# A third tile for layer 0's outputs, a store moved behind an activation, and four places in the order of layer 1's start changed

## The chip, the cores and the metric

The kernel runs on one NeuronCore of a Trainium2 chip. The metric is the device time of one execution in microseconds (us). The engines are named as the profile names them: PE (matrix multiply) with its weight loads PEld, DVE (vector), ACT (activation), POOL (GpSimd) and SP (which here only issues DMAs).

## The reference

The input x is fp32 of 4 images, 64 channels, 256 x 256. Two layers are computed, one after the other, each with a residual:

```python
    # --- layer 0 (conv_preact) ---
    x = x + _L0_conv_ref(_gn(x), ...)
    # --- layer 1 (conv_preact) ---
    x = x + _L1_conv_ref(_gn(x), ...)
```

`_gn` is a group norm over 32 groups of two channels: per image and group a mean and a variance over all pixels. Layer 0 is a 3x3 convolution with gelu, a 1x1 convolution to 128 channels that are split into xa and k, a 1x3 and a 3x1 depthwise convolution on xa with another gelu (the result is xs), a gate from the mean of xs over the image (softmax over three experts, the best two kept), three low-rank experts (ranks 2, 4 and 8) from k and xs, and a 1x1 projection:

```python
    h = _gelu(_conv2d(x, c1_w, ((1, 1), (1, 1))) + c1_b[None, :, None, None])
    h = _c1x1(h, c2_w, c2_b)
    xa, k = jnp.split(h, 2, axis=1)
    xs = _conv2d(xa, sh_w, ((0, 0), (1, 1)), groups=C) + sh_b[None, :, None, None]
    xs = _conv2d(xs, sv_w, ((1, 1), (0, 0)), groups=C) + sv_b[None, :, None, None]
    xs = _gelu(xs)
    ...
    return _c1x1(out, proj_w, proj_b)
```

Layer 1 is two 3x3 convolutions with quantized weights, each with a batch norm over all four images:

```python
    h = _conv3x3(x, _quantize_weight(w1), b1)
    h = jax.nn.relu(_batchnorm(h, gamma1, beta1))
    h = _conv3x3(h, _quantize_weight(w2), b2)
    h = _batchnorm(h, gamma2, beta2)
    return jax.nn.relu(h + identity)
```

## The kernel before

The work falls into stages. First the statistics of image 0 are read. Then the front runs: 64 units, 16 for each image, each of 16 rows of layer 0. A unit loads x (L548), takes differences of its rows on POOL and ACT, multiplies them on PE into `ps_c` (L532 through `front_conv`), combines the products on DVE (`butterfly_a` to `butterfly_d`, L650 to L669), applies gelu on ACT (L677) and runs the vertical taps on PE into `ps_a` in two halves (sub 0 and 1). For each half ACT writes t from ps_a (L718), DVE adds the horizontal taps in three steps (L725, L733, L736), ACT applies gelu to give xs (L749), and ACT issues the DMA that stores xs to DRAM (L754, `xs_store`). Every two units a product of h (`front_k`) and one of xs (`front_q`, L787) give the experts' low-rank values, which are stored too (L798).

The gate of an image is known only when all its xs are. So the outputs of image b are made 20 units later, inside the units of the next image (`plan_out`), 1 chunk of 16 rows (k from 0 to 15) per unit: SP loads xs (L865), the low ranks (L875) and x itself into a tile y (`out_load`, L855 and L856); PE projects into `ps_o` (`out_open`), in two halves n; DVE adds the projection to y (`out_add`, L901) and takes statistics of it (L906); SP stores y (`out_store`, L914). The y tiles have the tag "o" in the pool `work`, with two buffers, so the load of chunk k goes into the tile of chunk k - 2 and waits until that has been stored. While the front of image b runs, the statistics rows of image b + 1 are loaded as well (L429). The outputs of image 2 beyond the 22nd half and all of image 3 are made during layer 1 (`plan_out_late`).

The group norm of layer 1 is a chain of small steps with waits between the engines (`out_end`, through `group_norm`, `combine` and `root`): statistics are joined on DVE, PE sums them over partitions (`ps_m_y`, L283), DVE takes mean and differences (L285 to L290), PE sums again (`ps_v_y`, L293), DVE starts an inverse root (L296, L270, L271), POOL refines it in three steps (L275 to L277), and one operation makes the shift gn2[:, 2:3] (L924: on POOL for images 0 and 1, on DVE for 2 and 3). Each `next` of the chain has its own place in the order.

Layer 1's first convolution (`plan_conv1`) follows image by image, with 16 chunks and one last row each. For a chunk, SP loads the normalized-to-be rows yn (L933), POOL takes differences d (L362), ACT scales the odd rows in place and copies them (`conv1_upper_odd`, L951 and L378), ACT and DVE split the differences into two parts (L365, L372), DVE the odd rows (L381), PE multiplies them into `ps_hm` (odd) and `ps_h` (L315), ACT and DVE write the result h (L331, L337), ACT squares it for the batch norm (L401) and stores it. After the last chunk `conv1_end` (L1021) makes one more row, `ps_h_end`. Then comes the second convolution and a last pass over the output.

PSUM is cut into four banks of 4 KB per partition: two with the tag "c" (ps_c, ps_h), one "a" (ps_a, ps_hm) and one "p" (ps_o, ps_k, ps_q, ps_m_y, ps_v_y and others).

The order on every engine, and of the DMAs on SP and ACT, is written out by hand: `at(step, order, call)` enters a call under a step and an order within it, `at_slot(u, pos, call)` does it for a unit (two steps per unit), and all calls are run in sorted order with the scheduler told to keep that order on all five engines (L1320). `TAIL` gives the places of the units after the last one. The engines run in order: an instruction that waits holds all that stand behind it on its engine.

Of the kernel before, what the change touches and what calls it, by code (L numbers as in the profile page):

```python
# [9 lines left out]
F32 = mybir.dt.float32  # L10
# [4 lines left out]
ALU = mybir.AluOpType  # L15
# [5 lines left out]
P = 128  # L21
# [21 lines left out]
def conv_preact_kernel(ctx: ExitStack, tc: tile.TileContext, io, col128, colset, col64):  # L43
# [12 lines left out]
    def bank(tag, name):  # L56
        return psum.tile([P, 2, GP, W], F32, tag=tag, name=name, bufs=BANKS[tag])
# [53 lines left out]
    def chunk_out(name, tag, bufs):  # L111
        return work.tile([P, CPAIR, W], F32, tag=tag, name=name, bufs=bufs)
# [10 lines left out]

    eps = const.tile([P, 1], F32, name="eps")
    nc.vector.memset(eps, GN_EPS)
    eps_bn = const.tile([P, 1], F32, name="eps_bn")
    nc.vector.memset(eps_bn, BN_EPS)
    zeros = const.tile([P, PW], F32, name="zeros")
    nc.vector.memset(zeros, 0.0)
    m128 = const.tile([P, io["m128"].shape[1]], F32, name="m128")  # L130
# [1 line left out]
    def c128(name):  # L132
        return m128[:, col128[name][0] : col128[name][1]]
# [4 lines left out]
    av = lconst.tile([P, 3, C], F32, name="av")  # L138
    sv_sum, sh_sum, sh_bias, tap_bias = (column(n) for n in ("sv_sum", "sh_sum", "sh_bias", "tap_bias"))
    end, ends, edge_bias = column("end", 2), column("ends", 2), column("edge_bias", 2)  # L140
    outer = lconst.tile([P, 2, W], F32, name="outer")
    u_raw = lconst.tile([P, 6, 3, C], F32, name="u_raw")
    wk = lconst.tile([P, 2, 2, 32], F32, name="wk")
    both = lconst.tile([P, P], F32, name="both")
# [30 lines left out]
    def weights():  # L175

        m64_t = work.tile([P, 2, GF], F32, tag="xs", name="m64", bufs=4)
        m64 = flat(m64_t)[0:C, 0 : io["m64"].shape[1]]
        n = io["mc1"].shape[1]
        taps = flat(work.tile([P, 2 * GP, W], F32, tag="t", name="taps", bufs=1))[:, 0:n]  # L180
        nc.sync.dma_start(taps, io["mc1"])
        nc.sync.dma_start(m64, io["m64"])
        nc.sync.dma_start(m128, io["m128"])

        def c64(name):
            return m64[:, col64[name][0] : col64[name][1]]

        front_weights(taps)
        n = 9 * C
        nc.vector.tensor_tensor(flat(av), taps[:, n : n + 3 * C], taps[:, n + 3 * C : n + 6 * C], ALU.mult)  # L190

        nc.vector.tensor_reduce(sv_sum, c128("sv"), AX.X, ALU.add)
        nc.vector.tensor_reduce(sh_sum, sh, AX.X, ALU.add)
        nc.vector.tensor_scalar(sh_bias, sh_sum, c128("c2_ba"), c128("sh_b"), ALU.mult, ALU.add)
        nc.vector.tensor_scalar(tap_bias, sv_sum, sh_bias, c128("sv_b"), ALU.mult, ALU.add)
        for i in range(2):
            nc.vector.tensor_scalar(end[:, i : i + 1], sh[:, 2 * i : 2 * i + 1], c128("c2_ba"), None, ALU.mult)
        nc.vector.tensor_scalar(ends, end, sv_sum, None, ALU.mult)
        nc.vector.tensor_scalar(edge_bias, ends, -1.0, tap_bias, ALU.mult, ALU.add)
        for i in range(2):  # L200
            o = outer[:, i, :]
            nc.vector.tensor_scalar(o, zeros[:, 0:W], sh_bias, None, ALU.add)
            nc.vector.tensor_tensor(o[:, 0 : W : W - 1], o[:, 0 : W : W - 1], end, ALU.subtract)
            nc.vector.tensor_scalar(o, o, c128("sv")[:, 2 * i : 2 * i + 1], None, ALU.mult)

        nc.vector.memset(wk, 0.0)
        ps = small("ps_wk")
        nc.tensor.matmul(ps[:, 0:NLOW], c64("c2_k"), c64("w2_t")[:, 0:NLOW], start=True, stop=True)

        for s in range(2):  # L210
            half = slice(s * C, s * C + C)
            for i in range(2):
                o = 16 * i
                nc.vector.tensor_copy(wk[half, s, i, o : o + NLOW], ps[half, 0:NLOW])
        ps = small("ps_kb")
        nc.tensor.matmul(ps[:, 0:1], c64("w2_t"), c64("c2_bk"), start=True, stop=True)
        nc.vector.tensor_tensor(k_bias, ps[:, 0:1], c128("e_b2"), ALU.add)
        ps = small("ps_pw3")
        nc.tensor.matmul(ps[:, 0:C], c64("w3"), c64("proj_t")[:, 0:C], start=True, stop=True)
        nc.vector.tensor_copy(pw3, ps[:, 0:C])  # L220
        ps = small("ps_pb3")
        nc.tensor.matmul(ps[:, 0:3], c64("proj_t"), c64("b3"), start=True, stop=True)
        nc.vector.tensor_copy(pb3, ps[:, 0:3])
# [496 lines left out]
    def front_taps_h(u, sub):  # L720

        ps = open_a.pop((u, sub)).rearrange("p a b c -> p (a b) c")
        t = open_t[u, sub]
        edges = slice(0, W, W - 1)
        nc.vector.scalar_tensor_tensor(  # L725
            t[:, :, edges],
            ps[:, :, edges],
            sh[:, 1:2],
            edge_bias.unsqueeze(1).to_broadcast([P, 2 * GP, 2]),
            ALU.mult,  # L730
            ALU.add,
        )
        nc.vector.scalar_tensor_tensor(  # L733
            t[:, :, 1:W], ps[:, :, 0 : W - 1], sh[:, 0:1], t[:, :, 1:W], ALU.mult, ALU.add
        )
        nc.vector.scalar_tensor_tensor(  # L736
            t[:, :, 0 : W - 1], ps[:, :, 1:W], sh[:, 2:3], t[:, :, 0 : W - 1], ALU.mult, ALU.add
        )
        n = 2 * (u % NCH) + sub
        for at_n, i, row in ((0, 0, 0), (NOCT - 1, 1, 2 * GP - 1)):  # L740
            if n == at_n:
                rows = slice(i * C, i * C + C)
                nc.vector.tensor_tensor(t[rows, row, :], t[rows, row, :], outer[rows, i, :], ALU.subtract)

    def front_xs(u, sub):
        b, k = divmod(u, NCH)
# [105 lines left out]
        gate_engine.tensor_tensor(out_bias[b], row[:, 4:5], c128("proj_b"), ALU.add)  # L852

    def out_load(b, k):
        ys[b, k] = chunk_out(f"y_{b}_{k}", "o", 2)  # L855
        nc.sync.dma_start(flat(ys[b, k]), io["xp"][b, k])  # L856

    def xs_load(b, k, place):
# [161 lines left out]

    def conv1_end(b):  # L1021

        ps = bank("c", f"ps_h_{b}_end")
        convolve(ps[:, 0, 0, :], "w1", 0, diffs[(NCH - 1) % 2], CPAIR)
        h_out[b, NCH] = ps

# [51 lines left out]
    def at_each(places, chain):  # L1078
# [6 lines left out]
    SLOTS = UNITS + 3  # L1085

    TAIL = {
# [6 lines left out]
    }  # L1094
# [1 line left out]
    def at_slot(u, pos, call, *args):  # L1096

        step, order = (2 * u, pos) if pos < 6 else (2 * u + 1, pos - 6)
        if u >= UNITS:
            step, order = TAIL[u - UNITS, pos]  # L1100
            step += CONV1
        at(step, order, call, *args)

    def plan_front():
# [4 lines left out]
        for u in range(SLOTS):  # L1109
# [34 lines left out]
            if 0 <= u - 1 <= last:  # L1144
                at_slot(u, 7, front_taps_a, u - 1, 0)
                at_slot(u, 7.2, divide, u)
                at_slot(u, 9, front_taps_b, u - 1, 0)
                at_slot(u, 9.1, front_taps_i, u - 1, 0)
                at_slot(u + 1, 1.15, front_taps_h, u - 1, 0)
                at_slot(u + 1, 1.55, front_xs, u - 1, 0)  # L1150
                at_slot(u + 1, 1.6, xs_store, u - 1, 0)
            j = (u - 2) // 2
            alone = u < NCH + 4
            if u % 2 == 0 and 0 <= j < UNITS // 2:
# [104 lines left out]
    def plan_conv1(b):  # L1259
# [4 lines left out]
        for k in range(NCH):  # L1264
# [10 lines left out]

            at(load, 0, conv1_load, b, k)
            at(*late(diff, 13.08), conv1_differences, b, k)
            at(*late(odd, 13.36 if b == 0 and k == 3 else 13.1), conv1_upper_odd, b, k)
            behind = b == 0 and k == 1
            at(*late(up0, 13.36 if behind else 13.12), conv1_upper, b, k, 0)  # L1280
            at(*late(up1, 13.37 if behind else 13.14), conv1_upper, b, k, 1)
# [19 lines left out]
    for b in range(B):  # L1301
        if b < B - 1:
            plan_stats(b + 1)
            plan_out(b, NOCT if b < B - 2 else 22)
            if b == B - 2:
                plan_out_late(b, range(22, NOCT), [CONV1 + 16 + 4 * n for n in range(10)], 13.6, [(CONV1 + n, 12.6) for n in (56, 58, 58, 60, 60, 60, 61, 62)])
        else:
            t, e = CONV1 + 56, CONV1 + b * (NG + 1) - 10
            steps = [t + (e - 6 - t) * n // (NOCT - 1) for n in range(NOCT)]
            plan_out_late(b, range(NOCT), steps, 13.6, [(e - i, 15) for i in (5, 3, 3, 1, 1, 1, 0, -1)])  # L1310
        plan_conv1(b)

    kept_to = {
# [11 lines left out]
    def bn_affine(mv, gamma, beta, out, name):  # L1325

        ms = stat.tile([P, 2], F32, tag="ms", name=f"ms_{name}")
        for _ in combine(mv, B, c128("avg2"), eps_bn, ms, name):
            pass
        nc.vector.tensor_tensor(out[:, 0:1], ms[:, 1:2], c128(gamma), ALU.mult)  # L1330
        t = stat.tile([P, 1], F32, tag="s1", name=f"t_{name}")
        nc.vector.tensor_tensor(t, ms[:, 0:1], out[:, 0:1], ALU.mult)
        nc.vector.tensor_tensor(out[:, 1:2], c128(beta), t, ALU.subtract)
# [330 lines left out]
```

## Time and profile before

| what | us |
|---|---|
| median of 3 runs | 2936.22 |
| lowest and highest of them | 2935.35, 2952.88 |
| the profiled execution's own time | 2935.38 |
| its span | 2933.5 |
| PE busy | 2353.0 |
| DVE busy | 2435.1 |
| ACT busy | 1992.5 |
| POOL busy | 1693.0 |

The span is what the profile divides; 1.9 us of the execution's own time lie around it. The front's units run from about 62 to 1256 us, layer 1's first convolution from there to 1938, the second to 2497, the last pass to the end. Three kinds of views are used: windows (busy time of every engine in a stretch, with the granted clock, the share of time in which the 16 DMA engines were busy, and GB/s), the chain of waits (followed back from the last instruction of a window to what released it), and the timeline (instructions in order, with the idle time of the engine ahead of each in brackets and what ended it). Starts of the first butterfly operation on DVE (L650, once per unit) give the length of a unit.

### The profile page before, as it was taken

To read this page: it belongs to the slowest core of one execution; us is meant where nothing else is said; L and a number is where in the kernel's file an instruction comes from. 1 tells how busy PE (TensorE), PEld (TensorE's weight loads), DVE (VectorE), ACT (ScalarE), POOL (GpSimd) and SP (SyncE) were. 2 spreads that over 40 slices of the span, in tenths; PEclk is the share of its full clock that TensorE was granted. 3 is DMA by queue.
4 is the path that set the end of the run, shared out by engine and by line. 5 is a ranking of instruction groups with operands and counts; after the bars stand their busy time and mean duration, and the time that the engine had idled before them with its cause. 6 is when DMAs were issued, how large, how long until landed. Compare 5 with 4: busy or idle time off the path is not lost.

```text
span 2933.5 us, 52776 instructions
## 1 busy us (share of the span) xinstructions
PE 2353.0 (80%) x21576; PEld 1500.6 (51%) x21576; DVE 2435.1 (83%) x2818; ACT 1992.5 (68%) x2166; POOL 1693.0 (58%) x1315
## 2 busy tenths in 40 slices
PE   2999999999999999999899999989999999000000
PEld 1544445444445555456566667868888888000000
DVE  6788678888888988879998999879999898976664
ACT  4887887777775655576676677878888887432221
POOL 6999988787778888744454456735555564000000
PEclk9999999999999999999999999999999999555555
DMA  8665589999999999769999996657777764999999
GB/s 355 246 245 206 205 300 372 354 360 353 354 341 320 314 321 329 280 225 346 338 368 357 366 351 260 244 194 273 259 266 268 262 221 153 387 409 422 426 426 405
DMA packets 135715, 915.35 MB, mean 312 GB/s; under 512 B 14960, under 2 KB 15728, under 8 KB 40880
## 3 DMA queue, kind: packets, MB, share of 16 engines
q1 hardware_dynamic: 107824, 777.74, 71.3%
q10 hardware_dynamic: 27648, 134.23, 11.6%
q8 instruction: 170, 2.79, 0.4%
q14 instruction: 73, 0.60, 0.1%
HBM read 573.74 MB, written 338.17 MB: 311 GB/s over the span
## 4 chain that ended last, share of the span: by engine, by line
PE 48%; DMA 31%; DVE 11%; POOL 4%; ACT 3%; issue 2%; SPq 0%; ACTq 0%; DVEq 0%; POOLq 0%
PE ps_h L315 18%; PE ps_c L532 9%; DMA y<-in_xp 7%; DMA y_d<-y 6%; PE ps_h2m L315 6%; PE ps_a L532 6%; DMA y_end<-y_d 5%; DMA h<-h_d 4%; DMA out<-h 4%; PE ps_o L532 4%; PE ps_hm L315 3%; DMA yn<-y_d 3%; PE ps_q L787 1%; POOL x L580 1%; DVE y L901 1%
## 5 line engine op out<-in xcount | busy, mean ns | idle before, releaser
L315 PE MATMUL ps_h<-diff,w_q 128*128 128x512 f32 x3072 | 751.1, 399 | 7.6 <-DVE h L337 7.6
L315 PEld LDWEIGHTS ps_h<-diff,w_q 128*128 128x128 f32 x3072 | 574.3, 188 | 183.7 <-issue 24.5
L532 PE MATMUL ps_c<-v,us 64*64 64x256 f32 x9216 | 535.0, 380 | 13.8 <-DVE ps_c L663 11.3
L362 POOL TENSOR_TENSOR d<-yn 128x1024 f32<-128x1024 f32 x128 | 347.4, 2735 | 277.2 <-DMA yn<-y_d 181.1
L532 PEld LDWEIGHTS ps_c<-v,us 64*64 64x64 f32 x9216 | 358.7, 134 | 170.3 <-issue 15.8
L362 POOL TENSOR_TENSOR d<-h 128x1024 f32<-128x1024 f32 x126 | 307.7, 2464 | 206.5 <-DVE diff L370 136.9
L532 PE MATMUL ps_a<-h,av 64*64 64x512 f32 x4080 | 384.1, 490 | 35.4 <-DVE t L736 21.9
L337 DVE SCALAR_TENSOR_TENSOR h<-ps_h,scale_w,m 128x1024 f32<-128x1024 f32 x256 | 323.2, 1280 | 73.6 <-PE ps_h L315 59.3
L580 POOL TENSOR_TENSOR x<-x 128x512 f32<-128x512 f32 x256 | 328.9, 1285 | 12.8
L1526 ACT ACTIVATE h<-h,shift,gn 128x2048 f32<-128x2048 f32 (+1 forms) x65 | 134.3, 2067 | 274.5 <-DVE h L1525 269.9
L532 PEld LDWEIGHTS ps_a<-h,av 64*64 64x64 f32 x4080 | 152.9, 133 | 301.6 <-issue 194.6
L401 ACT ACTIVATE junk<-h,less_h 128x2048 bf16<-128x2048 f32 (+3 forms) x134 | 256.2, 1912 | 13.6 <-DVE h L337 13.5
L1525 DVE SCALAR_TENSOR_TENSOR h<-h,inverse,y_end 128x2048 f32<-128x2048 f32 (+1 forms) x65 | 150.5, 2317 | 120.5 <-DMA y_end<-y_d 120.5
L718 ACT ACTIVATE t<-ps_a,tap_bias,m 128x1016 f32<-128x1016 f32 x128 | 153.3, 1198 | 114.3 <-PE ps_a L532 85.2
L901 DVE SCALAR_TENSOR_TENSOR y<-ps_o,ob,y 128x1024 f32<-128x1024 f32 x128 | 163.9, 1280 | 50.7 <-PE ps_o L532 23.6
L749 ACT ACTIVATE xs<-t 128x1024 f32<-128x1024 f32 x128 | 134.8, 1053 | 104.0 <-DVE t L736 93.9
L315 PE MATMUL ps_h2m<-odd,w_q 128*128 128x512 f32 x768 | 193.2, 401 | 5.9 <-ACT odd L378 3.8
L315 PE MATMUL ps_hm<-odd,w_q 128*128 128x512 f32 x768 | 195.1, 404 | 2.8 <-DVE t L736 1.3
L372 DVE SCALAR_TENSOR_TENSOR diff<-d,gn,diff 128x1024 fp32r<-128x1024 f32 x128 | 192.7, 1536 | 0.0
L365 ACT ACTIVATE diff<-d 128x1024 fp32r<-128x1024 f32 x128 | 135.3, 1057 | 81.7 <-POOL d L362 80.1
L572 POOL TENSOR_TENSOR x<-x,x 128x512 f32<-128x512 f32 x128 | 160.8, 1278 | 21.3 <-ACT x L566 21.1
L315 PEld LDWEIGHTS ps_h2m<-odd,w_q 128*128 128x128 f32 x768 | 146.4, 191 | 42.6 <-ACT odd L378 3.9
(264 smaller groups left out, 4274.1 us busy)
## 6 DMA issues: line engine op xcount, KB each, us to landing
x<-in_xc SPq DMA_DIRECT2D x64, 1280.0 KB
h<-h_d SPq DMA_DIRECT2D x64, 1152.0 KB
yn<-y_d SPq DMA_DIRECT2D x60, 1152.0 KB
xs_in<-in_xp SPq DMA_DIRECT2D x64, 1024.0 KB
xs_d<-xs ACTq DMA_DIRECT2D x128, 512.0 KB
xs_in<-xs_d SPq DMA_DIRECT2D x64, 1024.0 KB
y<-in_xp SPq DMA_DIRECT2D x64, 1024.0 KB
y_d<-y SPq DMA_DIRECT2D x64, 1024.0 KB
```

Source lines behind the costliest of these rows:

```text
L315: nc.tensor.matmul(ps, wq[w][:, kind, kx, :], t[:, rows, kx : kx + W], start=(j == 0), stop=(j == len(terms) - 1))
L337: nc.vector.scalar_tensor_tensor(h.rearrange("p (e k) w -> p e (k w)", e=2), ps.rearrange("p e k w -> p e (k w)"), w_scale[w], m.unsqueeze ...
L362: engine.tensor_tensor(raw.rearrange("p (g r) w -> p g r w", g=2), *pair, ALU.subtract)
L365: nc.scalar.activation(inner(tiles[0], 4 * n, 4 * n + 4), raw, AF.Copy, scale=scale)
L372: nc.vector.scalar_tensor_tensor(lower, raw, scale, upper.bitcast(F32), ALU.mult, ALU.subtract)
L401: nc.scalar.activation(junk[rows, 0:n], flat(h), AF.Square, bias=less[name][rows], accum_out=total)
L532: last[:] = [nc.tensor.matmul(ps[o, at_out[0] : at_out[1], :], w[i], rhs[i], **flags)]
L572: nc.gpsimd.tensor_tensor(x4[:, j - 1], x_rows(u, j + 2), x4[:, j - 1], ALU.subtract)
L580: nc.gpsimd.tensor_tensor(x[:, r : r + 2], x[:, r + 2 : r + 4], x[:, r : r + 2], ALU.subtract)
L718: nc.scalar.activation(t[:, :, inside], ps[:, :, inside], AF.Identity, bias=tap_bias, scale=sh[:, 1:2])
L901: nc.vector.scalar_tensor_tensor(y, ps.rearrange("p x s w -> p x (s w)"), out_bias[b], y, ALU.add, ALU.add)
L1525: nc.vector.scalar_tensor_tensor(at_h, at_h, inverse[:, b : b + 1], y[:, a:e, :], ALU.mult, ALU.add)
```

## The change

Five edits and one tidying:

1. `out_load` takes every third chunk (k % 3 == 2) of images 0 and 1, and chunks 2, 5 and 8 of image 2, from a tile of its own with the tag "third" in the pool `front`, which has one buffer. The others stay on the two "o" tiles.
2. `xs_store` of the first half of a unit moves from place 1.6 of unit u + 1 to place 4.16, behind the second half's `front_taps_i` (4.15). `TAIL` is adapted.
3. `conv1_upper_odd` of image 0, chunk 0 moves from step t - 3 (unit 62's last places) to (t - 2, 4.2), inside unit 63, behind that unit's `front_taps_i`.
4. The chain of group norm 2 has its eight steps at 56, 60, 60, 64, 64, 66, 68 and 70 instead of 56, 58, 58, 60, 60, 60, 61 and 62; that of group norm 3 at e - 5, e - 2, e - 2, e + 1, e + 1, e + 1, e + 2 and e + 3 instead of e - 5, e - 3, e - 3, e - 1, e - 1, e - 1, e and e + 1.
5. `ps_h_end` goes to the bank "p" instead of "c".
6. `eps_bn` and `eps`, which are equal, become one tile; `outer` is kept as one row per partition, as only half of the partitions of each of its two rows was read.

Lines after L855 are three higher in the changed kernel (L924 becomes L927).

```diff
-    eps_bn = const.tile([P, 1], F32, name="eps_bn")
-    nc.vector.memset(eps_bn, BN_EPS)
...
-    outer = lconst.tile([P, 2, W], F32, name="outer")
+    outer = lconst.tile([P, W], F32, name="outer")
...
-                nc.vector.tensor_tensor(t[rows, row, :], t[rows, row, :], outer[rows, i, :], ALU.subtract)
+                nc.vector.tensor_tensor(t[rows, row, :], t[rows, row, :], outer[rows], ALU.subtract)
...
     def out_load(b, k):
-        ys[b, k] = chunk_out(f"y_{b}_{k}", "o", 2)
+        if k % 3 == 2 and (b < B - 2 or b == B - 2 and k < 11):
+            ys[b, k] = front_pool.tile([P, CPAIR, W], F32, tag="third", name=f"y_{b}_{k}")
+        else:
+            ys[b, k] = chunk_out(f"y_{b}_{k}", "o", 2)
         nc.sync.dma_start(flat(ys[b, k]), io["xp"][b, k])
...
     def conv1_end(b):
-        ps = bank("c", f"ps_h_{b}_end")
+        ps = bank("p", f"ps_h_{b}_end")
...
-        (0, 1.15): (0, 1.15), (0, 1.55): (0, 1.55), (0, 1.6): (0, 1.6), (0, 2): (0, 2), (0, 2.2): (0, 2.2),
+        (0, 1.15): (0, 1.15), (0, 1.55): (0, 1.55), (0, 4.16): (0, 1.6), (0, 2): (0, 2), (0, 2.2): (0, 2.2),
...
-        (1, 1.15): (3, 13.4), (1, 1.55): (3, 13.5), (1, 1.6): (4, 13.9), (1, 2): (5, 13.2), (1, 2.2): (5, 13.25),
+        (1, 1.15): (3, 13.4), (1, 1.55): (3, 13.5), (1, 4.16): (4, 13.9), (1, 2): (5, 13.2), (1, 2.2): (5, 13.25),
...
                 at_slot(u + 1, 1.55, front_xs, u - 1, 0)
-                at_slot(u + 1, 1.6, xs_store, u - 1, 0)
+                at_slot(u + 1, 4.16, xs_store, u - 1, 0)
...
-            at(*late(odd, 13.36 if b == 0 and k == 3 else 13.1), conv1_upper_odd, b, k)
+            at(*((t - 2, 4.2) if first else late(odd, 13.36 if b == 0 and k == 3 else 13.1)), conv1_upper_odd, b, k)
...
-                plan_out_late(b, range(22, NOCT), [CONV1 + 16 + 4 * n for n in range(10)], 13.6, [(CONV1 + n, 12.6) for n in (56, 58, 58, 60, 60, 60, 61, 62)])
+                plan_out_late(b, range(22, NOCT), [CONV1 + 16 + 4 * n for n in range(10)], 13.6, [(CONV1 + n, 12.6) for n in (56, 60, 60, 64, 64, 66, 68, 70)])
...
-            plan_out_late(b, range(NOCT), steps, 13.6, [(e - i, 15) for i in (5, 3, 3, 1, 1, 1, 0, -1)])
+            plan_out_late(b, range(NOCT), steps, 13.6, [(e - i, 15) for i in (5, 2, 2, -1, -1, -1, -2, -3)])
```

More of the change, by code (lines that the diff above doesn't have):

```diff
@@ L125, in conv_preact_kernel @@
     nc.vector.memset(eps, GN_EPS)
[L126 to L127 removed]
+    assert BN_EPS == GN_EPS
     zeros = const.tile([P, PW], F32, name="zeros")
@@ L200, in weights @@
         for i in range(2):
[L201 to L204, printed above, removed]
+            rows = slice(i * C, i * C + C)
+            o = outer[rows]
+            nc.vector.tensor_scalar(o, zeros[rows, 0:W], sh_bias[rows], None, ALU.add)
+            nc.vector.tensor_tensor(o[:, 0 : W : W - 1], o[:, 0 : W : W - 1], end[rows], ALU.subtract)
+            nc.vector.tensor_scalar(o, o, c128("sv")[rows, 2 * i : 2 * i + 1], None, ALU.mult)
         nc.vector.memset(wk, 0.0)
@@ L1327, in bn_affine @@
         ms = stat.tile([P, 2], F32, tag="ms", name=f"ms_{name}")
-        for _ in combine(mv, B, c128("avg2"), eps_bn, ms, name):
+        for _ in combine(mv, B, c128("avg2"), eps, ms, name):
             pass
```

## The prediction

> **What bounds the kernel now.** I read the page's busy shares and its slices first, since a share over the whole span mixes stages.
>
> ```profile
> PE 2353.0 (80%) x21576; PEld 1500.6 (51%) x21576; DVE 2435.1 (83%) x2818; ACT 1992.5 (68%) x2166; POOL 1693.0 (58%) x1315
> DMA  8665589999999999769999996657777764999999
> GB/s 355 246 245 206 205 300 372 354 360 353 354 341 320 314 321 329 280 225 346 338 368 357 366 351 260 244 194 273 259 266 268 262 221 153 387 409 422 426 426 405
> ```
>
> No engine is near 100%, but the DMA row has digits of 9 from the seventh slice on (a slice is 73 us), while the front still runs. The windows view of single stretches (PE, PEld, DVE, ACT, POOL busy, then clock, DMA share, GB/s) tells which stretch has which limit:
>
> ```profile
> 200.00:300.00 100.00, 96.19 (x1356) 50.54 (x1360) 80.43 (x122) 79.24 (x110) 90.16 (x78) 1.00 0.58 212
> 535.00:615.00 80.00, 75.43 (x1064) 39.71 (x1060) 66.54 (x91) 60.85 (x87) 62.74 (x68) 1.00 0.97 355
> 855.00:935.00 80.00, 79.73 (x1128) 40.85 (x1124) 70.55 (x94) 52.70 (x70) 66.40 (x72) 1.00 0.91 329
> 1300.00:1350.00 50.00, 49.80 (x242) 34.77 (x242) 44.66 (x63) 41.70 (x40) 25.15 (x11) 1.00 1.01 362
> 2500.00:2900.00 400.00, 0.00 (x0) 0.00 (x0) 281.97 (x134) 130.75 (x65) 0.00 (x0) 0.50 1.01 420
> ```
>
> From 855 on PE is full (79.73 of 80). At 535 to 615 PE is busy 75.43 of 80 and the DMA share is 0.97. Starts of one DVE operation per unit (L650) give the pace: from 426.8 to 863.4 us there are 22 units, 19.85 us each; just before and after, the chain has its PE pieces of ps_c 18.62 us apart (starts 404.08, 422.72, 441.33). So 22 x (19.85 - 18.62) = 27 us separate this stretch from PE's own pace, and no more can be won there. What ends last in it, the chain of waits says (start, length, what):
>
> ```profile
> 534.74 14.60 DMA y_d<-y
> 549.42 0.34 ACTq L754
> 549.81 1.21 ACT t L718
> ...
> 574.96 14.44 DMA y_d<-y
> 589.47 20.21 DMA y<-in_xp
> 609.76 1.28 DVE y L901
> ...
> 615.04 14.51 DMA y_d<-y
> ```
>
> Two things stand there. One is a loop over two `o` buffers: y store (14.4), y load into the same buffer (20.2), the add L901, and the store again, some 40 us for two units, which is what two units take. The other: at 549.42 ACT issues its xs store just as the y store of 534.74 lands. ACT sat behind a DMA completion, and t (L718) behind ACT.
>
> **The change part by part.** The sum goes against the profiled execution: span 2933.5, its own time 2935.4; the median of the runs shown is 2936.2, 0.8 above.
>
> *Third place for y, and xs store behind t (one gain, from units 21 to 43).* With three tiles in turn a y load no longer waits for the store two chunks before. SP waited 87.4 us for that in this stretch (L856 behind y_d, 21 times), but behind it SP waits for other things (L914 for the add L901, 84.3; L865, L429, L875 for other DMAs, 20 to 32 each), so only part moves forward. On DVE, L901 waited 14.7 us for y (9 times); on ACT, t waited 25.0 in 8 times under "PE ps_c" where the chain shows the DMA wait. These two are what can go: the store of the first half now stands behind the second half's t, where ACT's wait lies under DVE's three steps on t (0.23 + 1.28 + 1.28). All PE gaps of the stretch are 22.2 us, nearly all ps_a behind t. What is late next is the DMA itself: a unit moves 1280 + 4 x 1024 + 2 x 512 + 512 KB = 7.08 MB (page, part 6: x, stats rows, xs in, y, y_d, two xs halves, low ranks), which at PE's pace wants 380 GB/s. It has 355 at share 0.97, so some 366 at share 1, and 372 in the seventh slice: 19.0 to 19.3 us a unit. That is 0.5 to 0.85 us x 22 = 11 to 19 us if the queues never run dry. Ends: 0 (the pipe is the limit already) and -20 (372 GB/s kept). I take -10, below the middle, because the loads keep their order on SP behind the other waits. In units 43 to 62, PE is full and the same edit is worth 0. The xs store issues some 5 us later; its tile is reused two units (37 us) later, and the store lands 14 to 20 us after issue: hidden.
>
> The Trainium skill ("DMA: Bandwidth & Descriptors", section "Issuing engines are not separate DMA queues") says that transfers from SP and ACT share the same 16 engines, and that where they are issued only saves issue time. It speaks against this part: by it the stretch would keep its 355 GB/s and the sum would lose its -10. The share of 0.97 beside PE's 94% agrees with it halfway; the 0.03 left and the waits named above are what I count on.
>
> *Odd rows of layer 1 inside unit 63.* The timeline there:
>
> ```profile
> 1239.56 1.24 ACT L951 ACTIVATE yn<-yn,gn 128x1024 f32<-128x1024 f32 x1 [1.26 <-POOL d L362]
> 1242.40 0.70 DVE L650 TENSOR_TENSOR ps_c<-mc,ps_c 128x512 f32<-128x512 f32 x1 [2.22 <-ACT mc L645]
> 1246.66 4.22 PE L532 MATMUL ps_c<-v,us 64*64 64x256 f32 x48 [2.38 <-DVE ps_c L663]
> ```
>
> ACT waits 1.26 for POOL, does L951 and L378 (1.24 + 1.06), and only then mc, for which DVE and then PE wait; behind the 2.38 idle, 48 matmuls take 4.22 where they take 2.78 elsewhere (granted clock 0.69 in 1246 to 1251). The change puts L951 and L378 behind t. DVE then starts 2.2 earlier; PE's gap and slow restart are worth at most 2.38 + 1.44 = 3.8. Next late are the t steps and POOL's d, which PE waits for around 1268 (1.31) and 1291 (1.26), and the full pipe at 1300 to 1350 (share 1.01), so part is given back: -2.5 (0 to -3.8).
>
> *Chain of gn_2 spread (end of image 0 of layer 1).* Now PE waits at ps_m_y 1.86, ps_o 1.00, ps_v_y 2.82 (and 4.61 for 2.97 behind it), ps_h_end 1.26: 8.6 us. DVE sits 5.67 at L924. Afterwards L924 stands where POOL is long done (-5.67 on DVE), but ps_m_y and ps_v_y come right behind a ps_o, and ps_h_end too, all in the one `p` bank: each waits for the add L901. From DVE's rows (L901 1.28, behind L372 2.5 and L337 1.3) I get 3.7, 1.5 and 1.1, plus a slow restart of 1.5: 7.8. Between -1.5 and +2: 0.
>
> *Last row's bank, `c` to `p`.* At the end of image 1, ps_h_end waited 2.70 for DVE L337 and the next 12 matmuls took 4.14 instead of 2.97. In `p` it waits for L901 of the last output, done at 1627.26, so it starts 2.6 earlier; but the next ps_h waits for DVE's differences, which gain only the 0.27 wait and their order: -1.2 (-3.5 to 0). The skill ("Perfetto Trace Analysis", section "Optimizing Tensor Performance") wants independent matmul groups to rotate through banks, so that one is emptied while the next is filled. Going from two banks to a single one is against it, and by it this term would be 0 or a loss; here L901 ends before L337 does.
>
> *Chain of gn_3 later (start of image 3).* Now:
>
> ```profile
> 1783.85 10.89 POOL L362 TENSOR_TENSOR d<-yn 128x1024 f32<-128x1024 f32 x4
> 1784.32 0.20 DVE L924 TENSOR_SCALAR gn<-gn 128x1 f32<-128x1 f32 x1
> 1787.66 1.28 DVE L337 SCALAR_TENSOR_TENSOR h<-ps_h,scale_w,m 128x1024 f32<-128x1024 f32 x1
> 1790.04 1.24 ACT L951 ACTIVATE yn<-yn,gn 128x1024 f32<-128x1024 f32 x1 [3.73 <-POOL d L362]
> 1791.37 5.82 PE L315 MATMUL ps_h<-diff,w_q 128*128 128x512 f32 x24
> ```
>
> In the new order DVE's L271 comes behind d_15_0 (about 1785.0); POOL does two Newton steps (1.0 each), L939 (1 to 2.2), d_0_0 and d_0_1 (2.72 each), and only then the third step (0.9): 1794.4 to 1795.6. DVE's L924 waits for that, from about 1787 on, and behind it stand L337 of h_14 (1787.66 now, about 1795 then). PE's ps_h_15_0 waits for that bank: 1796.2 instead of 1791.4, and restarts slowly (+1.4). Given back: ps_h_end in `p` loses its 2.29 and the slow 4.50 behind it. From 1796.2: 4.4 + 2.9 for the two ps_h, 0.98, 2.97: ps_h_0_0 at 1807.3, now 1804.6: +2.7. A gap of 1.34 at ps_v_y (1776.9) goes, most of it under DVE. I take +2.5; ends -1 (DVE had slack) and +6 (nothing given back). PE is at 100% with the DMA at 0.72 behind this, so the loss stays.
>
> *Nothing:* one memset less, `outer` on halves (start, once), memory of the third tile (free before layer 1's pool opens), L951's new place at other images (none).
>
> Sum: -10 - 2.5 + 0 - 1.2 + 2.5 = -11.2: 2924.2 as profiled, 2925 as median.
>
> **Rivals.**
> *A: the pipe is the bound already.* For: 0.97 and 9s all along. Against: 1.01 at 1300. Then the front gives 0 to -3 and the rest -1.2: 2932 to 2935.
> *B: PE's full pace is reached.* For: both waits on the chain are taken away. Against: 380 GB/s were not seen in any front slice (372 at most). Then -27 - 1.2: 2908.
> *C: slower, by DVE's wait for POOL at 1787.* For: L924 is in order in front of h_14, POOL has 7.7 us of d_0 and L939 in front of its last step. Against: the two banks of `c` and ps_h_end in `p`. At its full price (+8, nothing given back) it decides when the front gives less than 6: with A, 2935.4 - 3.7 + 8 = 2940.
> *D: y is read from a tile whose place in SP's order is unchanged,* so it lands as late as before; only the xs store acts, half of the waits on the chain: -5 - 1.2: 2929.
>
> **How the numbers follow.** Forecast (front -6 to -16) 0.5: 2919 to 2929, 2925 as the likeliest. A 0.18, B 0.09, C 0.1, D 0.13. The range 2911 to 2938 leaves out B and the upper half of C, some 2 in 10 with what I have not thought of. The likeliest's own range is 2919 to 2929. About 1% (29 us) is what a measurement here tells from no change: faster by that needs more than B: 0.06; slower by that is out of reach of C: 0.03; within 1%: 0.91.
>
> **What would show it.** Pace of L650 between 427 and 863: 19.85 now, 19.4 by the forecast, 19.8 by A, 18.6 by B; GB/s there 364, 356, 380. SP's L856 no longer waiting for y_d. At unit 63 ps_c without a wait over 1 us, 48 matmuls in 2.8. DVE's L924 of gn_3 (L927 there) with an idle of 7 to 9 us behind POOL, and PE's ps_h idle 4 to 5 there. It is wrong if the pace stays and something else in SP's queue takes L856's place, or if the third image's start shows no idle of DVE.

## The result, and the profile after

| | before | changed kernel |
|---|---|---|
| median of 22 runs each, us | 2944.91 | 2943.93 |
| lowest and highest | 2935.35, 2952.98 | 2937.17, 2958.22 |
| ratio to before, 95% interval | | 1.0004 [0.9993, 1.0014] |
| profiled execution, own time and span | 2935.38, 2933.5 | 2941.94, 2939.8 |

No change in time can be told: the interval holds 1 (the quotient of the two medians is 0.9997). Of the three runs of before that the prediction had seen, two are the lowest of the 22, so their median, 2936.22, was low; the measured 2943.93 is above the forecast by 19 us, of which 8.7 are in the base and 10.2 in the change itself.

The two profiles, and all later ones, are compared by stretches. Each is the time between two starts on DVE: L650 of a unit (u), or L337 of the first convolution's n-th half chunk (h). "Before" is given for two profiles of it.

| stretch, us | before | changed | what lies there |
|---|---|---|---|
| u 0 to 18 | 310.7, 310.5 | 311.0 | front, PE bound |
| u 21 to 43 | 436.6, 436.8 | 441.7 | front with outputs and statistics loads |
| u 43 to 56 | 246.8, 246.8 | 247.5 | front, PE full |
| u 56 to h 0 | 160.2, 158.9 | 158.5 | unit 63's order |
| h 24 to 36 | 73.4, 72.9 | 72.3 | image 0's end, chain of gn_2 |
| h 56 to 72 | 88.5, 86.2 | 86.3 | image 1's end |
| h 88 to 96 | 39.9, 39.9 | 43.1 | image 3's start, chain of gn_3 |
| last h to the end | 439.3, 438.6 | 437.5 | second convolution's end, last pass |

The page of the changed kernel, in the lines that answer to those of before:

```profile
PE 2357.6 (80%) x21576; PEld 1498.7 (51%) x21576; DVE 2436.4 (83%) x2817; ACT 1991.8 (68%) x2166; POOL 1694.9 (58%) x1315
DMA  8665589999999999869999996647777764999999
GB/s 354 242 248 205 205 295 377 354 356 353 339 334 318 323 324 326 285 227 337 330 370 355 366 364 250 259 175 272 268 264 264 263 232 150 371 426 425 425 425 400
```

Hardly anything in it has moved. The windows view of a part of the stretch that was to gain (same columns as before):

```profile
535.00:615.00 80.00, 76.06 (x1068) 39.31 (x1064) 67.27 (x91) 60.73 (x87) 62.10 (x67) 1.00 0.96 352
```

352 GB/s where before had 355, and a share of 0.96 for 0.97. The y loads are free of the y stores. What SP waited for in units 21 to 43 (from 426 to 864 us; line, releaser, us in total, times, longest), first in the kernel before, then in the changed one, some rows of each:

```profile
SPq L856 <- DMA y_d<-y: 87.4, 21, 7.6
```

```profile
SPq L917 <- DVE y L904: 107.8, 22, 8.0
SPq L798 <- DMA ranks<-low_d: 32.2, 10, 4.8
...
SPq L859 <- DMA y<-in_xp: 23.8, 9, 3.1
...
SPq L548 <- DMA ranks<-low_d: 21.3, 9, 4.0
SPq L917 <- DMA y_d<-y: 21.0, 9, 2.8
...
SPq L859 <- DMA y_d<-y: 5.7, 1, 5.7
```

The wait of the y load for the y store is gone (87.4 us in 21 times before, one of 5.7 left). In its place stand waits of the y load, the low store, the x load and the y store for other DMAs that have not landed, and the y store waits longer for the add (107.8 us for 84.3). And DVE waits longer for y; the waits of the engines in the same window, before and changed:

```profile
ACT t L718 <- PE ps_a L532: 29.0, 28, 2.6
...
ACT t L718 <- PE ps_c L532: 25.0, 8, 3.4
...
DVE y L901 <- DMA y<-in_xp: 14.7, 9, 2.8
```

```profile
ACT t L718 <- PE ps_a L532: 43.9, 28, 3.3
DVE y L904 <- DMA y<-in_xp: 30.9, 10, 5.6
```

ACT's wait for a DMA ahead of t (25.0 us under "PE ps_c" before) has vanished as forecast, but t waits longer for ps_a (43.9 us for 29.0), and DVE waits 30.9 us for y, where it waited 14.7. The pace of units 21 to 43 is 441.7 / 22 = 20.08 us, not the 19.4 of the forecast: the pace did not fall and other DMAs took the place of L856's wait, which the prediction had named as the sign of its being wrong.

### The profile page after: what moved, and what is told of

The parts are those of the page before. It is cut to its first block, busy times and chain, and to the rows that moved or that the text cites. A ratio compares the mean times of both kernels' runs of the same rounds, so it can differ in the third digit from the quotient of the medians.

```text
span 2939.8 us, 52775 instructions
## 1 busy us (share of the span) xinstructions
PE 2357.6 (80%) x21576; PEld 1498.7 (51%) x21576; DVE 2436.4 (83%) x2817; ACT 1991.8 (68%) x2166; POOL 1694.9 (58%) x1315
## 3 DMA queue, kind: packets, MB, share of 16 engines
q8 instruction: 169, 2.77, 0.4%
## 4 chain that ended last, share of the span: by engine, by line
PE 47%; DMA 33%; DVE 10%; POOL 4%; ACT 3%; issue 2%; SPq 0%; ACTq 0%; DVEq 0%; POOLq 0%
PE ps_h L315 19%; DMA y<-in_xp 13%; PE ps_c L532 8%; PE ps_h2m L315 6%; PE ps_a L532 5%; DMA out<-h 4%; DMA y_end<-y_d 4%; PE ps_o L532 3%; DMA h<-h_d 3%; DMA yn<-y_d 3%; DMA y_d<-y 3%; PE ps_hm L315 3%; DMA xs_in<-in_xp 1%; POOL x L580 1%; DVE h L1536 1%
## 5 line engine op out<-in xcount | busy, mean ns | idle before, releaser
L315 PEld LDWEIGHTS ps_h<-diff,w_q 128*128 128x128 f32 x3072 | 577.2, 189 | 191.2 <-issue 19.7
L532 PE MATMUL ps_a<-h,av 64*64 64x512 f32 x4080 | 383.7, 489 | 27.2 <-DVE t L736 10.9
L337 DVE SCALAR_TENSOR_TENSOR h<-ps_h,scale_w,m 128x1024 f32<-128x1024 f32 x256 | 322.8, 1279 | 64.6 <-PE ps_h L315 51.5
L904 DVE SCALAR_TENSOR_TENSOR y<-ps_o,ob,y 128x1024 f32<-128x1024 f32 x128 | 164.0, 1281 | 76.2 <-DMA y<-in_xp 30.9
```

The source lines that it names most:

```text
L315: nc.tensor.matmul(ps, wq[w][:, kind, kx, :], t[:, rows, kx : kx + W], start=(j == 0), stop=(j == len(terms) - 1))
L337: nc.vector.scalar_tensor_tensor(h.rearrange("p (e k) w -> p e (k w)", e=2), ps.rearrange("p e k w -> p e (k w)"), w_scale[w], m.unsqueeze ...
L532: last[:] = [nc.tensor.matmul(ps[o, at_out[0] : at_out[1], :], w[i], rhs[i], **flags)]
L904: nc.vector.scalar_tensor_tensor(y, ps.rearrange("p x s w -> p x (s w)"), out_bias[b], y, ALU.add, ALU.add)
```

## The experiments

All times are ratios to runs of the kernel before on the same chip. "Stretch" is the time of units 21 to 43 in the one profile of each kernel, GB/s that of the window 430 to 840 us.

| kernel | ratio, 95% interval | stretch, us | GB/s |
|---|---|---|---|
| before, two profiles | | 436.6, 436.8 | 356, 357 |
| changed | 1.0004 [0.9993, 1.0014] | 441.7 | 352 |
| e1, statistics loads split | 1.0027 [1.0012, 1.0041] | 439.5 | 354 |
| e2, half statistics | 0.9946 [0.9926, 0.9966] | 418.9 | 345 |
| e3, chain of gn_3 as before | 0.9998 [0.9979, 1.0018] | 445.0 | 350 |
| e4, two y tiles | 1.0021 [1.0003, 1.0038] | 441.6 | 354 |
| e5, xs store as before | 0.9999 [0.9979, 1.0018] | 434.5 | 359 |
| e7, statistics earlier, gn_3 as before | 0.9985 [0.9971, 0.9999] | 427.1 | 352 |
| e8, three places as before | 1.0029 [1.0013, 1.0046] | 434.9 | 358 |
| e9, before with half statistics | 0.9939 [0.9920, 0.9958] | 420.8 | 344 |
| e10, y load first | 0.9990 [0.9976, 1.0004] | 433.7 | 359 |
| e11, e7 with xs store as before | 0.9963 [0.9945, 0.9981] | 424.9 | 355 |
| e12, gn_3 and xs store as before | 0.9996 [0.9979, 1.0013] | 435.9 | 358 |
| e13, before with statistics earlier | 0.9981 [0.9967, 0.9994] | 434.9 | 345 |
| e14, before with the later xs store | 1.0016 [1.0003, 1.0028] | 437.5 | 357 |
| e15, e13 with the third tile | 0.9970 [0.9958, 0.9983] | 424.8 | 355 |
| e16, e13 again | 0.9970 [0.9953, 0.9987] | 429.0 | 351 |

Three theories of the stretch were held against each other: *pipe* (the bytes that the DMA engines move are the bound), *in-flight* (the number of DMAs under way is the bound, since each waits for one issued eight before), and *loop* (the two y tiles are the bound, as the prediction had it). For *in-flight*: the DMAs carry eight semaphores in turn, and the waits of a DMA for another one that the trace of the changed kernel tells in this stretch (47 of them) are all for one issued seven to nine places before.

**Bytes or number of DMAs: e1 and e2.** e1 cuts the statistics loads of images 2 and 3 into two DMAs each, e2 leaves out the second of the two and takes the statistics of the first half twice, so that the engines do the same work.

```diff
+        n = CPAIR * W // 2 if b >= 2 else CPAIR * W
+        for a in range(0, CPAIR * W, n):
+            nc.sync.dma_start(flat(x_in[b, k])[:, a : a + n], io["xp"][b, k][:, a : a + n])
```

> The changed kernel, with every load of statistics rows of images 2 and 3 (units 12 to 43) cut into two DMAs of half a row each: one DMA more per unit (9.5 for 8.5), the same bytes. Theory pipe (units 21 to 43 are bound by the bytes that the 16 DMA engines move, some 355 GB/s): pace stays 20.0 to 20.2 us a unit, time within 5 us of the changed kernel. Theory in-flight (the trace shows that a DMA is issued only when the one issued eight before it has landed; that is what took the place of the y wait): eight in flight cover less, so 5 to 12% longer units: +20 to +50 us.

> The changed kernel, with only the first half of each load of statistics rows of images 2 and 3 (it leaves out half of these rows, the statistics are taken over the other half twice): 512 KB of 6912 KB less per unit in units 12 to 43, the same number of DMAs, waits and engine work. Theory pipe: 6.55 MB at 355 to 366 GB/s is 17.9 to 18.5 us, below PE's 18.62, so the stretch falls to PE's pace: -25 to -33 us, about 2912. Theory in-flight: one DMA of seventeen lands some 6 us earlier every second wait, the others as before: -3 to -10 us.

With one DMA more per unit the stretch took 439.5 us, not longer than the changed kernel's 441.7, where *in-flight* asked for 20 us more: it is out. (The whole of e1 is 0.0023 above the changed kernel; its profile has 1.6 us of that in units 0 to 18 and as much in 18 to 21, and 4.7 in the last pass, which e1 does not touch.) With 512 KB less per unit the stretch fell by 22.8 us. The windows view of e2 from 430 to 840 us, and of the changed kernel, the same:

```profile
430.00:840.00 410.00, 404.74 (x5672) 207.85 (x5664) 361.63 (x467) 330.88 (x467) 341.44 (x349) 1.00 0.96 345
```

```profile
430.00:840.00 410.00, 390.22 (x5415) 198.52 (x5404) 343.05 (x445) 316.15 (x446) 325.98 (x335) 0.99 0.97 352
```

PE is busy 404.74 of 410 in e2 and 390.22 in the changed kernel; the GB/s go down because PE now sets the pace. Note the share: 0.96 at 345 GB/s, 0.97 at 352. It does not tell which of the two kernels is bound by the pipe.

**Was the y loop ever a bound: e9 and e4.** e9 is the kernel before, with two y tiles, and e2's cut. e4 is the changed kernel without the third tile.

```diff
-        if k % 3 == 2 and (b < B - 2 or b == B - 2 and k < 11):
-            ys[b, k] = front_pool.tile([P, CPAIR, W], F32, tag="third", name=f"y_{b}_{k}")
-        else:
-            ys[b, k] = chunk_out(f"y_{b}_{k}", "o", 2)
+        ys[b, k] = chunk_out(f"y_{b}_{k}", "o", 2)
```

> The kernel before (two y tiles, early xs store), with only the first half of each load of statistics rows of images 2 and 3 (it leaves out half of these rows). Theory pipe: the loop of y store, y load and add was only the place where the full pipe showed; with 512 KB less per unit it shrinks by itself, and units 21 to 43 take 419 to 422 us as in the changed kernel with the same cut: -16 to -18 us. Theory loop (two tiles bind, whatever the bytes): the loop's 40 us for two units stays within 1 us, 430 us or more for the stretch, and the third tile is worth 10 us here: -5 us at most.

> The changed kernel, with all y tiles on the two old places. Theory pipe: the third place is worth nothing, time and pace of units 21 to 43 (20.0 to 20.2 us) stay, within 4 us. Rival (the third place helps and another edit of the front, the later xs store, costs as much): +5 to +10 us. Second rival (a third tile makes the queue deeper and so slower): -5 us, pace back to 19.85.

e4's stretch is the changed kernel's (441.6 and 441.7); the whole of e4 is 0.0017 above the changed kernel, with intervals that overlap, and this stretch does not show why. e9 falls to 420.8 us, and it still has the loop. The wait of its SP for y stores and the windows view, both from 430 to 840 us:

```profile
SPq L858 <- DMA y_d<-y: 86.0, 21, 7.0
```

```profile
430.00:840.00 410.00, 402.76 (x5664) 209.68 (x5660) 359.31 (x464) 329.61 (x466) 338.49 (x347) 1.00 0.95 344
```

SP waits 86.0 us for the y stores, no less than the kernel before does in this window (79.8 us in 20 times), with PE at 402.76 of 410, where before has this:

```profile
430.00:840.00 410.00, 388.84 (x5444) 199.20 (x5440) 344.45 (x448) 317.68 (x447) 328.45 (x338) 1.00 0.97 356
```

So this wait, read off the chain as the thing to remove, costs next to nothing. The transfers of the loop hardly became shorter in e9 (stores of 13.3 to 13.9 us and loads of 19.7 to 20.2 in its chain, 14.3 to 14.6 and 19.9 to 20.8 before), but the chain leaves it: y loads and y stores are 33.5% of the chain from 500 to 700 us in e9, and 87.0% of that from 480 to 640 in the kernel before.

**The y load's place in SP's order: e10.** `at_slot(u - 1, 2.0, out_load, b, k)` becomes `at_slot(u - 1, 0.1, ...)`.

> The changed kernel, with the y load first in SP's order of a unit, ahead of the loads of low ranks, xs and statistics rows instead of behind them (rival D of the prediction: y has lain at the same place of SP's order, so it landed as late as before). Theory pipe: y lands earlier, another load later, stretch of units 21 to 43 within 434 to 446 us, time within 4 us of the changed kernel. Rival D: DVE no longer waits for y (30.9 us there) and the stretch falls by 5 to 10 us.

DVE no longer waits for the y load, as rival D wanted, and the stretch is 433.7 us, 8.0 less than the changed kernel's, which is the size that rival D named. But other things come later in return: ACT's t waits 55.7 us for ps_a (426 to 864 us), and PE 10.9 us for xs rows (430 to 840 us). Nor do 8 us of one profile decide: e3 and e8, which run the changed kernel's program up to unit 62, took 445.0 and 434.9 us. The ratio's interval holds 1; a gain of more than 0.24% on the kernel before is excluded, a smaller one is not.

**The xs store: e5, e12 and e14.** e5 and e12 take the store back to place 1.6 (e12 the chain of gn_3 too), e14 makes that edit alone on the kernel before.

```diff
-                at_slot(u + 1, 4.16, xs_store, u - 1, 0)
+                at_slot(u + 1, 1.6, xs_store, u - 1, 0)
```

> The changed kernel, with the first half's xs store back ahead of the second half's t. Theory pipe (bytes bound units 21 to 43): the stretch from unit 21 to 43 stays at 437 to 445 us and the time within 4 us of the changed kernel, though ACT's wait for a DMA ahead of t comes back. Rival 1 (ACT's wait was a real cost): +5 to +8 us. Rival 2 (the later store has made the queue worse, as the stretch was 436.6 us before and 441.7 after): -5 us, 436 us for the stretch.

> The changed kernel with two edits undone, those that the runs speak against: group norm 3's chain at its old places and the xs store ahead of t. By the profiles: -3 for the chain, 0 to -7 for the store: 0.997 to 1.000 of the time before. Rival (the difference of 434.5 and 441.7 us was scatter and the chain's stall is given back later): 1.000.

> The kernel before with one edit only: the first half's xs store behind t. Theory pipe without a cost of the late store: 436 us for units 21 to 43 (436.6 and 436.8 in the two profiles of before), time within 2 us. Rival (the late store itself is what costs, as the profiles with it had 441.6 to 445.0 us and once 434.9): 440 us or more and 1.001 to 1.003.

By e14 alone the later store costs 0.16% (interval from 0.03 to 0.28), though its stretch, 437.5 us, is not the 440 that this theory named. By e12, which has the third tile and not the later store, there is no gain on before. The stretch without the later store scatters from 434.5 to 436.8 us (four profiles with all bytes in the order of before) and with it from 433.7 to 445.0. That the store costs some us there is likely; how many is not settled. What it does to the waits is plain. In e14, from 426 to 864 us:

```profile
ACT t L718 <- PE ps_a L532: 43.1, 31, 2.7
DVE y L901 <- DMA y<-in_xp: 26.8, 10, 4.1
```

So the longer waits of the changed kernel (43.9 and 30.9) come with this edit alone, with two y tiles; e5 and e12, with the third tile and without the edit, have 31.3 and 30.7 ahead of t and 15.5 and 14.9 ahead of the add, as before. Ahead of t this holds in all profiles with all bytes: 39.8 to 55.7 us with the later store, 29.0 to 31.3 without. The wait for y is less sure (with the edit, e8 has 19.5 and e1 14.8). The later store has taken away ACT's wait for a DMA and put other waits in its place. Behind this stretch its price is clear of scatter: units 43 to 56 take 247.5 to 247.8 us in the nine profiles with the later store and 246.8 or 246.9 in the nine without, and from unit 56 to 63 it is 0.5 us more.

**How far a profile scatters: e6.**

> The kernel before, unchanged, for a second profile: how far the stretch of units 21 to 43 scatters by itself. If 436.6 and 441.7 us differ only by scatter, this one may lie anywhere between 434 and 445 us; if the change made the stretch longer, it lies within 2 us of 436.6.

436.8 beside 436.6 us for the stretch. These two lie close, but one program differs by more elsewhere: 434.9 and 429.0 us in e13 and e16, one kernel on two chips, and 441.7, 445.0 and 434.9 in the changed kernel, e3 and e8, which are the same up to unit 62. So in units 21 to 43 a difference of less than 10 us between single profiles tells nothing. The last pass, the same in every kernel, took from 435.9 to 446.6 us over all profiles.

**The chain of gn_3: e3.** The places of before in the changed kernel:

```diff
-[(e - i, 15) for i in (5, 2, 2, -1, -1, -1, -2, -3)]
+[(e - i, 15) for i in (5, 3, 3, 1, 1, 1, 0, -1)]
```

> The changed kernel, with the chain of group norm 3 at its old places. My step (DVE's shift operation waits 8.4 us behind POOL's differences, PE 4.9 us and a slow restart): the stretch from h 88 of layer 1's first convolution to h 96 loses 3 us, total -3. Rival (the stall lies beside other waits): 0. DVE's idle ahead of the shift operation of gn_3 goes in both.

h 88 to 96 went back from 43.1 to 39.9 us, and is 39.9 to 40.1 in every kernel with the old places and 43.0 to 43.4 in every one with the new. In the changed kernel:

```profile
1798.83 0.21 DVE L927 TENSOR_SCALAR gn<-gn 128x1 f32<-128x1 f32 x1 [8.36 <-POOL gn L277]
1798.96 1.28 DVE L337 SCALAR_TENSOR_TENSOR h<-ps_h,scale_w,m 128x1024 f32<-128x1024 f32 x1
```

```profile
1793.22 4.69 POOL L362 TENSOR_TENSOR d<-yn 128x1024 f32<-128x1024 f32 x2
1797.90 0.34 POOL L275 TENSOR_SCALAR root_y<-var_y,gn 128x1 f32<-128x1 f32 x1
```

```profile
1800.30 8.01 PE L315 MATMUL ps_h<-diff,w_q 128*128 128x512 f32 x24 [4.86 <-DVE h L337]
```

Read from below: PE waits 4.86 us for DVE's h, DVE stands 8.36 us at a 0.21 us operation, because POOL does two differences of 2.35 us each ahead of the last step of the root. The whole-time ratio (0.9998 for 1.0004) has the right sign and cannot tell 3 us.

**The three other places: e8.** Unit 63's odd rows, the last row's bank and the chain of gn_2 as before, in the changed kernel.

```diff
-            at(*((t - 2, 4.2) if first else late(odd, ...)), conv1_upper_odd, b, k)
+            at(*late(odd, ...), conv1_upper_odd, b, k)
-    ps = bank("p", f"ps_h_{b}_end")
+    ps = bank("c", f"ps_h_{b}_end")
-    (56, 60, 60, 64, 64, 66, 68, 70)
+    (56, 58, 58, 60, 60, 60, 61, 62)
```

> The changed kernel with three edits undone: layer 1's first odd rows behind unit 62 again, the last row in bank c, group norm 2's chain at its old places. By my steps: unit 56 to unit 63 takes 132 us (130.3 in the changed kernel), image 1's end from h 56 to h 72 88.5 (86.3), image 0's end from h 24 to h 36 73.4 (72.2): in sum +4 to +5 us. Rival (what is won there is waited for later): each of the three shows locally, but the time stays within 2 us.

u 56 to h 0 took 159.4 us (158.5 in the changed kernel), h 24 to 36 74.1 (72.3), h 56 to 72 87.2 (86.3): +3.6 in the three. The time says +0.25% (1.0029 for 1.0004, intervals that just touch). All profiles together, eight with the old places and ten with the new, say it better: 158.9 to 160.6 us for u 56 to h 0 with the old and 157.9 to 158.5 with the new, clear of scatter, and a gain of 1.6 by the means of kernels whose xs store is at the same place; 72.8 to 75.0 and 72.3 to 73.8 for h 24 to 36, 86.1 to 88.7 and 85.1 to 88.2 for h 56 to 72, where the means differ by 0.4 and 0.9 and the ranges overlap.

**A version that is faster: e7, e11, e13, e15, e16.** If bytes bind, fewer must be asked for in units 21 to 43. Image 2's statistics are read in units 12 to 23, where the DMA engines have room at first (in the kernel before a share of 0.55 and 209 GB/s from 265 to 373 us, units 12 to 18, then 0.93 and 332 up to 464), and image 3's over units 23 to 43:

```diff
-    PARTS = (4, 2, 1, 1)
+    PARTS = (4, 2, 2, 1)
...
-        t = NCH * (b - 1) - (4 if b > 1 else -1)
-        per = 11 / NCH if b == 1 else 1
+        t = (0, 1, 12, 23)[b]
+        per = (0, 11, 11, 20)[b] / NCH
```

> The changed kernel with group norm 3's chain at its old places, and with the statistics of image 2 read at the pace and with the split between ACT and DVE of image 1 (units 12 to 23 in place of 12 to 28), those of image 3 over units 23 to 43 in place of 28 to 44: the same bytes in all, 0.2 MB less per unit in units 23 to 43, more in units 12 to 23, where the DMA share is below 0.9 at first. Theory pipe: about 0.5 to 0.7 us less per unit in units 23 to 43, some given back in 18 to 23: -6 to -12 us, 2930 to 2935. Rival (latency and waits bind, not bytes): 0. Rival (ACT, at 0.79 in units 8 to 14, becomes the bound in 12 to 18): +5 us.

> The version with statistics of images 2 and 3 read earlier and group norm 3's chain at its old places, with the xs store back ahead of t as well. Theory pipe: 6.87 MB per unit at 355 GB/s, 425 to 428 us for units 21 to 43, as with the late store (427.1); time -3 to -6 us against before. Rival (the late store costs something, as 434.5 against 441.7 us in one profile suggests): 3 to 7 us less than that, -8 us.

> The kernel before with one edit only: the statistics of image 2 read in units 12 to 23 and those of image 3 over units 23 to 43, as in the version that was 0.9963 of the time before. Theory pipe: that version's gain is this edit's alone, 0.995 to 0.998, and units 21 to 43 take 424 to 429 us. Rival (two y tiles still cost something there): 430 us or more for the stretch, 0.998 to 1.000.

> The kernel before with two edits: statistics of images 2 and 3 read earlier, and the third y tile (with the smaller outer tile that makes room for it). Theory pipe alone: as with the statistics alone, 0.998 of the time before, 430 to 436 us for units 21 to 43 if 434.9 was right. Theory pipe and loop (with fewer bytes per unit the two tiles are the next limit, and the third takes it away): 424 to 429 us, 8 to 10 us less, and 0.995 to 0.997.

> The kernel with the earlier statistics alone and two y tiles, once more beside the one with three on the same chip. If the 434.9 us of units 21 to 43 was scatter, this one has 424 to 430; if the two tiles bind there, 432 to 437, and its time lies 3 to 10 us above that with three.

e11 beats both kernels: 0.9963 of before. Units 0 to 21 give 1.5 us back (up to 3.8 in the other profiles with this edit), units 21 to 43 win 12. The last two ran side by side, with and without the third tile: the stretch is 424.8 and 429.0 us (434.9 in e13, the same kernel as e16), the time 0.9970 in both. So with fewer bytes two tiles take 4 to 10 us more in the stretch, in these profiles, which is no more than one program's scatter, and no difference in time can be told; the earlier statistics alone carry the gain. What e15 and e16 differ by is not settled below 5 us.

## Why the prediction was wrong

- **Third tile and later xs store, -10: failed.** The prediction put the two waits on the chain as the thing in the way and the pipe's limit at 366 to 372 GB/s. Both waits went (others took their place, some of them brought by the later store itself), and no time came: with all bytes, 350 to 359 GB/s is what the stretch moves, whatever waits (eleven profiles with the statistics at their old places and full). The step that failed is "355 at share 0.97, so some 366 at share 1": the share does not scale so (0.96 at 345 GB/s, 0.97 at 359, and 1.01 both at 362, from 1300 to 1350 us before, and at 424 in the last pass). The 372 of one slice was a peak beside slices of 354. Rival A was right, and e2 and e9 show its cause, the bytes. A smaller step failed with it: in units 43 to 62 the later store was put at nothing, and it costs 0.7 us from unit 43 to 56 and 0.5 from there to 63.
- **PE's pace, 18.62: mis-sized.** The spacing of pieces in the chain was taken for the mean. Units 43 to 56, PE full, take 246.8 / 13 = 18.98 us, and e2 has 418.9 / 22 = 19.04. At most 19 us could be won, not 27, and rival B's 2908 was out of reach.
- **Unit 63, -2.5: right in kind, smaller.** ACT's wait and the two odd-row operations are gone from the front of mc, and 48 matmuls of ps_c follow a 0.56 us wait where it had been 2.38:

```profile
1248.27 0.60 ACT L645 ACTIVATE mc<-ps_c 128x512 f32<-128x512 f32 x1 [1.99 <-PE ps_c L532]
1251.82 2.83 PE L532 MATMUL ps_c<-v,us 64*64 64x256 f32 x48 [0.56 <-DVE ps_c L663]
1255.63 2.38 PE L532 MATMUL ps_a<-h,av 64*64 64x512 f32 x24 [0.98 <-DVE t L736]
```

  2.83 us for the 48, as forecast. The start of unit 63 comes 2.3 us earlier (unit 56 to 63 takes 129.8 to 130.3 us in all profiles with the new place and 132.1 to 132.6 with the old). Up to h 0 the gain is 1.6 us by the means; t, named as late next, takes a part (0.98 us in the last row).
- **Chain of gn_2, 0 between -1.5 and +2: held.** PE waits 2.04 ahead of ps_m_y and 2.77 ahead of ps_v_y for the add, as forecast, and 1.00 ahead of ps_h_end, for DVE's variance (L296) and not for the add; with the 12 slower matmuls behind it (4.40 us for 2.97) that is 7.2 us for the 7.8 of the forecast. The stretch differs by 0.4 us in the means, which is within the scatter.
- **Last row's bank, -1.2: held where it can be seen.** At image 1's end ps_h_end now starts right behind ps_h, without the 2.70 wait, and the 12 matmuls after it take 3.02 for 4.14. h 56 to 72 takes 86.3 us; before it was 88.5 and 86.2, and the means of all profiles differ by 0.9, so the size is within the scatter. The advice of the Trainium skill that the prediction named ("Perfetto Trace Analysis", section "Optimizing Tensor Performance"), to rotate independent matmul groups through banks, did not bite here: in the single bank ps_h_end starts without a wait.
- **Chain of gn_3, +2.5: right.** Forecast: DVE idle 7 to 9 us, PE 4 to 5; measured 8.36 and 4.86, and 3.2 us in the stretch.
- **The sum.** Without the -10 the prediction's own terms make -1.2 us, 0.9996; measured 1.0004 [0.9993, 1.0014]. With what the stretches show in place of these terms (-1.6, -0.4, -0.9, +3.2, and +1.2 for the later store in units 43 to 63) it is +1.5 us, 1.0005, without units 21 to 43, whose scatter is larger; so close to the measured ratio it is by luck. Single edits of 2 to 5 us can't be told by the time here, only in their place.

Rival C's mechanism was there at the price of the forecast, not at its full 8; rival D described the y load's place correctly (between 690 and 800 us it is issued within 3 us of before), but e10, with the load first, shows no gain in time (0.9990 [0.9976, 1.0004]) and a stretch 8.0 us shorter within a scatter of 10; whether the place is worth some us stays open.

## What to carry to other kernels

A wait that fills the chain may be only the place where a full resource shows. Before a buffer is added for it, take bytes away and leave the wait, or split a transfer and leave the bytes. Two runs told here that the bytes were worth 16 to 18 us (e2 and e9, 0.9946 and 0.9939), and that the wait for the y store can stay (e9). In a stretch that is bound by traffic, look for a neighbour with room and move loads there.

An operation of 0.2 us in the order of a full engine costs what its producer is late: DVE stood 8.36 us, because POOL's step had two long operations placed in front of it. When steps of a chain are spread out, look what each engine has between them.

## What the runs showed of the hardware

- The DMA share is not a measure of room. The same 0.95 to 0.97 stood over 344 to 359 GB/s, with the pipe or with PE as the bound, and 1.01 stood over 362 GB/s from 1300 to 1350 us (before) as over 411 to 424 in the last pass. Why the stretch stops at 350 to 359 stays open: more DMAs of half the size (e1) did not change it. The Trainium skill ("DMA: Bandwidth & Descriptors", section "Where 436 GB/s comes from") gives about 358 GB/s as a core's share of HBM and 435 as the ceiling of the fabric, and lets the first bind transfers between HBM and SBUF; the stretch lies at the first figure, the last pass of the same runs at 411 to 424, so no run here shows that figure to be the reason.
- The last pass is the same in all kernels and its rate is not. From 2520 to 2900 us it moves 424 GB/s in e16 and 411 in e11, both at a share of 1.01, and from the last h on these are 435.9 and 446.6 us. This scatter of 10 us is half of the 18 to 21 us between the lowest and highest run, and is why small edits were read by stretches.
- PE can slow after short waits. Behind the 4.86 us idle, 24 matmuls took 8.01 us instead of 5.8, with a granted clock of 0.51 from 1798 to 1804 us; behind 2.38 us in the kernel before it was 0.69 from 1246 to 1251, and 48 matmuls took 4.22 us instead of 2.8. Behind 2.04 us ahead of ps_m_y in the changed kernel 12 matmuls took 3.06 us, hardly more than the 2.97 elsewhere. The skill ("TensorE: Matmul & The Clock Gate", section "What's actually happening") has the clock halved after an idle window of about 3.4 us; the first case agrees, the second came after a shorter wait.
